# Moving filler work and VectorE's side work between the steps of a hand-ordered decoder layer

## The chip, the cores and the metric

The kernel runs on one core of one Trainium2 chip. The metric is the device time of one execution in microseconds (us); the time of a kernel is the median over its runs. The profile is of one further execution, recorded by the hardware profiler.

## The reference

One transformer layer in fp32 on 16 sequences of 512 tokens with 256 features. Cut to what matters:

```python
q = query @ wq + query @ Aq @ Bq * 4      # k, v alike; 16 heads of 16 features
q, k = rope(q), rope(k)
attn = softmax(where(causal, -1e9, q @ k.T / 4))
x = layernorm(query + (attn @ v) @ wo)
h = butterfly(x @ W_exp + b_exp, up_weights)        # 10 stages on 1024 features
h = butterfly(gelu(h + up_bias), down_weights)
out = layernorm(x + h @ W_con + b_con + down_bias)
```

Both butterflies are linear, so the kernel folds them into the two matrices once, in the first steps, and then computes `gelu(x @ W1 + b) @ W2`.

## The kernel before

The work is cut into steps, and the order of every engine's work is written out by hand. A batch (one sequence) takes 20 steps, `per = PER_QUAD * NQ`, in four quads of five steps; a quad is half of the heads of one chunk `c` of 128 features (`par` 0 or 1). A step has a slot 0 to 4 within its quad. Slots 0 and 1 treat 512 columns of scores for a pair of heads, slots 2 and 3 treat 384 + 128, slot 4 treats 256 + 256 for both pairs.

Two streams run through the steps, the second 15 steps (three quads) behind the first:

- `largest` computes scores into the PSUM tile `pa` (L421) and VectorE reduces each row of them to its largest (L430, the tiles `junk` and `mx`). One reduction is two instructions: a custom operation that reads the scores and a short read of the accumulator.
- `weights` computes transposed scores into `pb` (L479); ScalarE takes the exponential into `pT` (L493) and GpSimd zeroes the part above the diagonal (L497).

`pa` and `pb` have one buffer each, so TensorE can write the next step's scores only when VectorE and ScalarE have read those of this one. In slot 4 both tiles hold scores of both streams. After the scores of a step TensorE gets other work, which fills the time until the tiles are free again. Such fillers are:

- `weigh` (L521): probabilities times v, into `po`.
- `project_v` (L383): the product that makes v of one 128-token tile, into `pvv`; ScalarE copies it out (L391), in the last batch VectorE does.
- `contract` (L660): one half (four of eight chunks) of the second feed-forward product of a token tile, into `py`. After the second half VectorE adds the residual (L668) and takes the statistics (L577, L578).
- `project_out` (L559): the attention's output product, into `pwo`; VectorE adds the residual (L567) and takes the statistics.
- `hidden` (L633), `project` (L337) and the transposes `turn_x1` (L616) and `place_largest` (L448, tile `ptm`).

All filler tiles share three PSUM banks (`ps_w`).

VectorE's side work hangs on the same steps. `normalize(b, c, t)` inverts the softmax sums of one token tile (L553) and multiplies the attention output by them (L554); `project_out` of that tile needs the result. `spread` (L589, then a power on GpSimd, L590) and `offset` (L595) turn the statistics into scale and offset of the layer norm, which `centre` applies on ScalarE (L602).

GpSimd also does the rotary products and sums of the batch that comes next (L362, L365, L367 in `turn`), one per step, behind its L497 of that step.

`add(step, f, ...)` appends a function to the list `others[step]`. In a step come first the scores of both streams, then the reductions and exponentials, then `weigh`, then `others[step]` in the order of appending, then `holes[step]`. Each engine runs its instructions in that order. Batches are scheduled one after the other in a loop, so what an earlier batch put into a step stands ahead of what a later one puts there. In that loop `s` is the first step of batch `b`, and the tuples `at` are steps relative to it. A step relative to `s` modulo 20 is its place in the batch, and modulo 5 its slot.

Of the kernel before, what the change touches and what calls it, by code (L numbers as in the profile page):

```python
# [17 lines left out]
P = 128  # L18
# [15 lines left out]
def decoder_layer(  # L34
# [18 lines left out]
    nc = tc.nc  # L53
    B, T, D = x.shape
# [405 lines left out]
    state = {}  # L460
# [86 lines left out]
            nc.sync.dma_start(rows_of(sums, 1), rows_of(x, 0))  # L547
            nc.sync.dma_start(rows_of(even, 1), rows_of(x, 1))

    def normalize(b, c, t):  # L550
        x, sums = state["heads", b, c]
        ts = slice(t * P, (t + 1) * P)
        nc.vector.reciprocal(sums[:, ts], sums[:, ts])  # L553
        nc.vector.tensor_tensor(x[:, ts], x[:, ts], sums[:, ts], ALU.mult)  # L554

    def project_out(b, t):
        pw = bank(f"pwo_{b}_{t}", [P, D])
        for c in range(NC):
            nc.tensor.matmul(  # L559
                pw,  # L560
                state["heads", b, c][0][:, t * P : (t + 1) * P],
                wo_sb[:, c, :],
                start=(c == 0),
                stop=(c == NC - 1),
            )
        z = zs[b]
        nc.vector.tensor_add(z[:, t, :], pw, z[:, t, :])  # L567
        stats_of(1, b, t)
# [23 lines left out]
    def offset(which, b, t0=0, t1=NT):  # L592
        stats, norm = state["stats", which, b], state["norm", which, b]
        ts = slice(t0, t1)
        nc.vector.scalar_tensor_tensor(  # L595
            norm[:, 2, ts], stats[:, ts, 0], -1.0, norm[:, 1, ts], ALU.mult, ALU.mult
        )
# [30 lines left out]
    def hidden(b, hc, fused=False):  # L628
        if hc == 0:
            state["h", b] = hpool.tile([P, NHC, T], F32, tag="h", name=f"h_{b}")  # L630
        ph = bank(f"ph_{b}_{hc}", [P, T])
        for c in range(NC):
            nc.tensor.matmul(  # L633
                ph,
                wup[:, c, hc * P : (hc + 1) * P],
                state["x1T", b][:, c, :],
                start=(c == 0),
                stop=(c == NC - 1),
            )
        h = state["h", b][:, hc, :]  # L640
        if fused:
            nc.scalar.activation(h, ph, AF.Gelu, bias=hbias[:, hc : hc + 1])
        elif hc % 4 == 0:
            nc.vector.tensor_copy(h, ph)
        else:
            nc.scalar.copy(h, ph)  # L646

    def gelus(b, count=NHC):
        h = state["h", b]
        for hc in range(count):  # L650
            nc.scalar.activation(
                h[:, hc, :], h[:, hc, :], AF.Gelu, bias=hbias[:, hc : hc + 1]
            )
# [36 lines left out]
    others = {s: [] for s in range(-head, last)}  # L690
# [3 lines left out]
    def add(s, f, *args):  # L694
        others[s].append(lambda: f(*args))

    def start_projection(b, side, c):
        state["pr", b, side, c] = project(b, side, c)
# [13 lines left out]
    for b in range(B):  # L712
        s = b * per
        if b > 0:

            at = {1: (-16, -11, -13, -9), B - 1: (-1, 4, 10, 10)}.get(b, (-3, -1, 4, 14))
            for t in range(NT):
                add(s + at[t], project_v, b, t)
        if b + 1 < B:

            add(s - head * (b == 0), load_xT, b + 1)
            at = {0: (2, 5, 7, 10), 1: (3, 6, 8, 11)}.get(b, (10, 10, 10, 10))
            for i, (c, side) in enumerate(chains):
                holes.setdefault(s + at[i], []).append(
                    lambda b=b, side=side, c=c: start_projection(b + 1, side, c)
                )
                turning = s + max(at[0] + 1 + 3 * i, at[i] + 1)
                for step in range(3):
                    add(turning + step, turn, b + 1, side, c, step)
                for step in range(1 + side):  # L730
                    add(turning + (6 if i == 3 else 4) + step, part, b + 1, side, c, step)
        add(s + 9, load_x, b)
        add(s + 11, place_largest, b, 0)
        add(s + 21, place_largest, b, 1)
        for c in range(NC if b + 1 < B else 1):
            for t in range(NT):
                at = (27, 28, 29, 31) if c == 0 else (36, 37, 39, 40)
                add(s + (at[t] if b + 1 < B else 29 + t), normalize, b, c, t)
        if b + 1 < B:
            for t in range(NT):  # L740
                add(s + 41 + t // 2, project_out, b, t)
            add(s + 42, spread, 1, b)
            add(s + 43, offset, 1, b)
            add(s + 44, centre, 1, b)
            for c in range(NC):
                add(s + 45 + (b + 2 == B), turn_x1, b, c)
        if b + 2 < B:

            late = 2 * (b + 3 == B)
            for hc in range(NHC - late):  # L750
                add(s + 46 + hc // 2, hidden, b, hc)
            holes.setdefault(s + 50, []).insert(0, lambda b=b, late=late: gelus(b, NHC - late))
            for hc in range(NHC - late, NHC):
                holes[s + 50].append(lambda b=b, hc=hc: hidden(b, hc, True))
            for t in range(NT):
                for half in range(2):
                    at = (11, 12, 13, 15, 16, 18, 20, 23)[2 * t + half]
                    if b + 3 == B and t == NT - 1:
                        at = (23, 25)[half]
                    add(s + 40 + at, contract, b, t, half)  # L760
            add(s + 63 + 2 * (b + 3 == B), spread, 2, b)
            add(s + 67, offset, 2, b)
            add(s + 68, centre, 2, b)
            add(s + 68, store, b)
# [15 lines left out]
    for t in range(NT):  # L780
        add(end + 2, normalize, z, NC - 1, t)
# [206 lines left out]
```

## Time and profile before

| | |
|---|---|
| runs | 1358.62, 1364.54, 1364.14 us |
| median | 1364.14 us |
| profiled execution | 1357.15 us |
| its span | 1355.4 us |
| TensorE clock granted | 0.993 |
| TensorE busy | 1320.3 us, 97% of the span |
| TensorE weight loads | 702.5 us, 52% |
| VectorE busy | 925.8 us, 68% |
| ScalarE busy | 707.3 us, 52% |
| GpSimd busy | 510.9 us, 38% |
| DMA | 63.49 MB, 47 GB/s on average |

In lines of the timeline the first number is the start in us from the beginning of the span, the second the duration in us, then engine, source line, operation, and output and input tiles with their sizes; x2 means two merged instructions, whose common time is given. A bracket names idle time of the engine before the line and what ended it. PE is TensorE, PEld its weight loads, DVE VectorE, ACT ScalarE, POOL GpSimd. A matmul's displayed end is modelled and overlaps the next one's start, so lengths of steps are taken from start to start. On VectorE an instruction is often shown to start some 0.08 us ahead of the end of the one before it. The chain of waits is followed back from the last instruction, at each step to what released it.

### The profile page before, as it was taken

How to read it: one execution, taken by the hardware profiler on the slowest of the kernel's cores; microseconds unless marked ns; L12 is line 12 of the kernel's file. 1: busy time of each engine (PE TensorE's matmuls, PEld its weight loads, DVE VectorE, ACT ScalarE, POOL GpSimd, SP SyncE). 2: the span in 40 equal slices, each digit the busy share in tenths (PEclk: the TensorE clock that was granted, in tenths of full speed). 3: DMA queues.
4: the chain of work that ended last, by engine and by line, in shares of the span. 5: the costliest groups of instructions: out<-in, count | busy, mean ns of one | idle time of the engine just before them, and what ended most of it. 6: DMA issues, size and time to landing. Idle time of an engine off the chain costs nothing.

```text
span 1355.4 us, 23859 instructions
## 1 busy us (share of the span) xinstructions
PE 1320.3 (97%) x8728; PEld 702.5 (52%) x8728; DVE 925.8 (68%) x2949; ACT 707.3 (52%) x1079; POOL 510.9 (38%) x777
## 2 busy tenths in 40 slices
PE   8898999999999999999999999999999999998998
PEld 4453545455454545555454554545555454554555
DVE  4788757667685766758577685857768685776632
ACT  2575454454646445464645545464554546445643
POOL 3534215344251533425153352515335252531311
PEclk9998999999999999999999999999999999999999
DMA  5311010110102011010110101010110101000000
GB/s 172 120 45 45 22 59 30 40 45 30 68 30 74 30 41 45 30 67 30 67 35 31 57 30 68 30 60 30 40 60 30 68 30 55 30 27 32 30 12 31
DMA packets 45685, 63.49 MB, mean 47 GB/s; under 512 B 5752, under 2 KB 26232, under 8 KB 45568
## 3 DMA queue, kind: packets, MB, share of 16 engines
q1 hardware_dynamic: 41680, 56.42, 11.8%
q10 hardware_dynamic: 3888, 5.55, 1.3%
q8 instruction: 69, 1.13, 0.3%
q14 instruction: 48, 0.39, 0.1%
HBM read 23.40 MB, written 8.91 MB: 24 GB/s over the span
## 4 chain that ended last, share of the span: by engine, by line
PE 84%; DVE 11%; ACT 3%; issue 2%; DMA 0%; POOLq 0%; POOL 0%; DVEq 0%; SPq 0%; ACTq 0%
PE pb L479 19%; PE ph L633 17%; PE py L660 16%; PE po L521 10%; PE pqk L337 8%; DVE junk L430 5%; PE pvv L383 4%; PE pwo L559 3%; PE pa L421 3%; DVE bn L577 1%; PE pb L421 1%; PE pt L616 1%; ACT pT L493 1%; PE pa L479 1%; DVE z L567 1%
## 5 line engine op out<-in xcount | busy, mean ns | idle before, releaser
L430 DVE CUSTOM_DVE_ANT_0 junk<-pa,causal 128x384 bf16<-128x384 f32 (+2 forms) x878 | 438.3, 499 | 235.0 <-PE pa L421 176.1
L493 ACT ACTIVATE pT<-pb 128x1024 f32<-128x1024 f32 (+1 forms) x314 | 293.8, 936 | 377.3 <-PE pa L421 227.6
L497 POOL TENSOR_SCALAR_AFFINE_SELECT pT<-pT 128x256 f32<-128x256 f32 x512 | 202.5, 407 | 733.3 <-ACT pT L493 731.6
L479 PE MATMUL pb<-qz,kz 17*128 17x512 f32 (+2 forms) x1756 | 328.8, 473 | 16.1 <-ACT pT L493 12.1
L421 PE MATMUL pa<-kz,qz 32*128 32x384 f32 (+3 forms) x1756 | 329.2, 474 | 4.2 <-DVE mx L430 4.2
L660 PE MATMUL py<-wdn,h 128*128 128x256 f32 x1024 | 252.1, 391 | 0.0
L479 PEld LDWEIGHTS pb<-qz,kz 17*128 17x128 f32 (+1 forms) x1756 | 142.9, 183 | 179.5 <-issue 82.2
L633 PE MATMUL ph<-x1T,yb 128*128 128x512 f32 x512 | 235.8, 604 | 0.0
L660 PEld LDWEIGHTS py<-wdn,h 128*128 128x128 f32 x1024 | 185.1, 189 | 72.2 <-issue 36.2
L521 PE MATMUL po<-pT,vaug 128*32 128x512 f32 (+3 forms) x2048 | 179.5, 446 | 0.0
L633 PEld LDWEIGHTS ph<-x1T,yb 128*128 128x128 f32 x512 | 92.4, 189 | 122.3 <-issue 97.6
L421 PEld LDWEIGHTS pa<-kz,qz 32*128 32x128 f32 (+1 forms) x1756 | 143.7, 184 | 13.6 <-DVE mx L430 11.2
L553 DVE RECIPROCAL sums<-sums 128x128 f32<-128x128 f32 x128 | 121.1, 946 | 0.0
L337 PE MATMUL pqk<-xT,wqk 128*128 128x512 f32 x256 | 118.5, 613 | 0.0
L646 ACT COPY h<-ph 128x512 f32<-128x512 f32 x84 | 49.2, 585 | 123.2 <-PE ph L633 123.2
L521 PEld LDWEIGHTS po<-pT,vaug 128*32 128x32 f32 x2048 | 47.1, 109 | 102.3 <-issue 78.2
L430 DVE DVE_READ_ACCUMULATOR2_ANT mx<- 128x1 f32 x1024 | 84.5, 82 | 0.0
L337 PEld LDWEIGHTS pqk<-xT,wqk 128*128 128x128 f32 x256 | 48.0, 194 | 61.9 <-issue 57.4
L365 POOL TENSOR_TENSOR swap<-swap,rope_sb 128x512 f32<-128x512 f32 x62 | 79.6, 1283 | 0.0
L602 ACT ACTIVATE z<-z,norm 128x256 f32<-128x256 f32 x128 | 66.7, 589 | 24.6 <-DVE norm L595 24.5
L668 DVE TENSOR_TENSOR z<-py,z 128x256 f32<-128x256 f32 x64 | 27.1, 423 | 74.1 <-PE py L660 73.9
L430 DVE CUSTOM_DVE_ANT_0 junk<-pb,causal 128x256 bf16<-128x256 f32 (+3 forms) x146 | 63.6, 436 | 17.3 <-PE pa L421 4.0
(91 smaller groups left out, 1334.2 us busy)
## 6 DMA issues: line engine op xcount, KB each, us to landing
xT<-in_xT SPq DMA_DIRECT2D x16, 512.0 KB
swap<-qz SPq DMA_DIRECT2D x64, 128.0 KB
swap<-kz SPq DMA_DIRECT2D x64, 128.0 KB
z<-in_x SPq DMA_DIRECT2D x16, 512.0 KB
sums<-x SPq DMA_DIRECT2D x64, 128.0 KB
out_y<-z SPq DMA_DIRECT2D x15, 512.0 KB
x<-x SPq DMA_DIRECT2D x32, 128.0 KB
early<-in_wexpT ACTq DMA_DIRECT2D x1, 1028.0 KB
```

Source lines behind the costliest of these rows:

```text
L337: nc.tensor.matmul(pq, wqk[:, d, e : e + P], xTs[b][:, d, :], start=(d == 0), stop=(d == NC - 1))
L365: engine.tensor_tensor(swap, swap, rope_sb[:, 1, :], ALU.mult)
L421: lambda i=i, rows=rows, at=at, n=n, t=t, ps=ps: nc.tensor.matmul(ps[:, i, at : at + n], q[rows, par, t * P : n], k_[rows, par, 0:n], star ...
L430: lambda i=i, at=at, n=n, t=t, g=g, ps=ps: nc.vector.tensor_tensor_reduce(out=junk[:, 0:n], in0=ps[:, i, at : at + n], in1=causal[:, T - n ...
L479: lambda i=i, rows=rows, at=at, n=n, k=block, ps=ps: nc.tensor.matmul(ps[:, i, at : at + n], kt[rows, par, k * P : (k + 1) * P], qt[rows, ...
L493: nc.scalar.activation(pT[:, heads, 0:n], ps[:, :, at : at + n], AF.Exp)
L497: nc.gpsimd.affine_select(out=diag, in_=diag, pattern=[[0, 2], [1, P]], compare_op=ALU.is_ge, fill=0.0, base=0, channel_multiplier=-1,)
L521: nc.tensor.matmul(po[HG * g : HG * (g + 1), k * P : T], vaugs[b % 2][:, k, NG * c + g, first : first + HG], pT[:, g, at : at + n], start= ...
L553: nc.vector.reciprocal(sums[:, ts], sums[:, ts])
L602: nc.scalar.activation(zs[b][:, t, :], zs[b][:, t, :], AF.Identity, bias=norm[:, 2, t : t + 1], scale=norm[:, 1, t : t + 1],)
L633: nc.tensor.matmul(ph, wup[:, c, hc * P : (hc + 1) * P], state["x1T", b][:, c, :], start=(c == 0), stop=(c == NC - 1),)
L660: nc.tensor.matmul(py, state["h", b][:, hc, t * P : (t + 1) * P], wdn[:, hc, :], start=(hc == 0), stop=(hc == NHC - 1),)
```

## The change

Four tuples of places are changed, `normalize` is split in two, and one function moves to the front of its step.

- v products: for most batches token tile 1 moves from step -1 to 0 and tile 3 from 14 to 12; for the last batch tile 0 moves from -1 to -3.
- Contraction halves: from places 11, 12, 13, 15, 16, 18, 0, 3 to places 11, 13, 14, 15, 16, 18, 19, 3 (steps 51 to 63 after the batch's first).
- Reciprocal and product: `invert` and `scale` are scheduled apart. For `c` = 0, token tile 3 moves from step 31 to 30. For `c` = 1 the reciprocals stay at 36, 37, 39, 40 and the products move to 39, 39, 40, 41, behind the reductions of these steps; 41 is also the step of the first two `project_out`.
- `offset(1, b)` is put first in step 43's list, so that VectorE runs it ahead of the residual add and statistics of `contract` (of an earlier batch), instead of behind them.

No operation is added or removed.

```diff
-    def normalize(b, c, t):
+    def invert(b, c, t):
+        sums = state["heads", b, c][1]
+        ts = slice(t * P, (t + 1) * P)
+        nc.vector.reciprocal(sums[:, ts], sums[:, ts])
+
+    def scale(b, c, t):
         x, sums = state["heads", b, c]
         ts = slice(t * P, (t + 1) * P)
-        nc.vector.reciprocal(sums[:, ts], sums[:, ts])
         nc.vector.tensor_tensor(x[:, ts], x[:, ts], sums[:, ts], ALU.mult)
+
+    def normalize(b, c, t):
+        invert(b, c, t)
+        scale(b, c, t)
...
-            at = {1: (-16, -11, -13, -9), B - 1: (-1, 4, 10, 10)}.get(b, (-3, -1, 4, 14))
+            at = {1: (-16, -11, -13, -9), B - 1: (-3, 4, 10, 10)}.get(b, (-3, 0, 4, 12))
             for t in range(NT):
                 add(s + at[t], project_v, b, t)
...
             for t in range(NT):
-                at = (27, 28, 29, 31) if c == 0 else (36, 37, 39, 40)
-                add(s + (at[t] if b + 1 < B else 29 + t), normalize, b, c, t)
+                if b + 1 == B:
+                    add(s + 29 + t, normalize, b, c, t)
+                    continue
+                add(s + ((27, 28, 29, 30), (36, 37, 39, 40))[c][t], invert, b, c, t)
+                add(s + ((27, 28, 29, 30), (39, 39, 40, 41))[c][t], scale, b, c, t)
         if b + 1 < B:
             for t in range(NT):
                 add(s + 41 + t // 2, project_out, b, t)
             add(s + 42, spread, 1, b)
-            add(s + 43, offset, 1, b)
+            others[s + 43].insert(0, lambda b=b: offset(1, b))
             add(s + 44, centre, 1, b)
...
             for t in range(NT):
                 for half in range(2):
-                    at = (11, 12, 13, 15, 16, 18, 20, 23)[2 * t + half]
+                    at = (11, 13, 14, 15, 16, 18, 19, 23)[2 * t + half]
                     if b + 3 == B and t == NT - 1:
                         at = (23, 25)[half]
                     add(s + 40 + at, contract, b, t, half)
```

## The prediction

> **What bounds the kernel now.** I read the chain of waits first, then TensorE's timeline over one batch in the middle of the run, then VectorE's and GpSimd's beside it.
>
> ```profile
> PE 84%; DVE 11%; ACT 3%; issue 2%; DMA 0%; POOLq 0%; POOL 0%; DVEq 0%; SPq 0%; ACTq 0%
> ```
>
> The chain of waits is TensorE with a tenth of VectorE in it: TensorE is nearly always fed, and stops where a score bank is still being read. I number the 20 steps of a batch as places 0 to 19 (step modulo 20; slot = place modulo 5). A step starts with its first `pb` product. TensorE's timeline at places 14 to 16:
>
> ```profile
> 608.51 1.13 PE L383 MATMUL pvv<-wv_sb,xT 128*128 128x256 f32 x4
> 609.67 0.70 PE L479 MATMUL pb<-qz,kz 17*128 17x512 f32 x2
> 609.80 0.70 PE L421 MATMUL pa<-kz,qz 32*128 32x512 f32 x2
> ...
> 611.42 1.99 PE L660 MATMUL py<-wdn,h 128*128 128x256 f32 x8
> 613.35 0.70 PE L479 MATMUL pb<-qz,kz 17*128 17x512 f32 x2
> 613.36 0.70 PE L421 MATMUL pa<-kz,qz 32*128 32x512 f32 x2
> ```
>
> After a v product in a last slot the next step comes 609.67 - 608.51 = 1.16 us later, 1.06 where nothing waits (618.42 to 619.48, place 17), and `pa` trails `pb` by 0.13 instead of 0.01. So such a boundary costs 0.10 + 0.12 us. A contraction half fills 613.35 - 611.42 = 1.93 us and leaves no gap. Now VectorE and GpSimd around place 1:
>
> ```profile
> 628.50 0.95 DVE L553 RECIPROCAL sums<-sums 128x128 f32<-128x128 f32 x1
> 628.55 1.27 POOL L362 TENSOR_TENSOR kz<-kz,rope_sb 128x512 f32<-128x512 f32 x1
> ...
> 629.48 0.48 DVE L554 TENSOR_TENSOR x<-x,sums 128x128 f32<-128x128 f32 x1
> ...
> 632.12 0.42 DVE L567 TENSOR_TENSOR z<-pwo,z 128x256 f32<-128x256 f32 x1
> 632.18 1.27 POOL L365 TENSOR_TENSOR swap<-swap,rope_sb 128x512 f32<-128x512 f32 x1
> ...
> 632.60 0.28 PE L448 MATMUL ptm<-ident,mx 128*32 128x128 f32 x1
> ```
>
> Two things matter here. `ptm` shares the bank of `pwo` t=0 and starts 0.06 us after L567 ends: L567 is on TensorE's path. And the product L554 takes 0.48 us here, while alone (665.37) it takes 0.29. It ends 0.14 after GpSimd's rope product at 628.55 (629.96 against 629.82). At 679.32 the same product meets a rope product that runs from 678.87 to 680.14:
>
> ```profile
> 679.32 0.97 DVE L554 TENSOR_TENSOR x<-x,sums 128x128 f32<-128x128 f32 x1
> ```
>
> It ends at 680.29, again 0.15 after GpSimd. So a VectorE operation with two SBUF inputs does not slow down beside a rope product, it stops until that ends; the reciprocal, one input, keeps 0.95 in both cases. The tiny offset L595, also two SBUF inputs, shows it most clearly:
>
> ```profile
> 1276.23 2.32 DVE L595 SCALAR_TENSOR_TENSOR norm<-stats,norm 128x4 f32<-128x4 f32 x1
> ```
>
> Its usual 0.15 became 2.32 beside L621 on GpSimd (1276.17, 2.37). Before the change the reciprocal ahead of each product covers most of a rope product; the product loses only some 0.2.
>
> **The change part by part.** Times within a step are from its start.
>
> *Contraction and v products, places 12, 14, 15.* Place 12 goes from 4.00 (599.31 to 603.31) to place 17's 3.13, which has the same content. Place 14 from 3.36 to 0.12 stall + 1.08 scores + 1.00 weighing + 1.93 = 4.13. Place 15 from 3.68 to 3.56, its 0.12 stall gone. 10.82 for 11.04: -0.22 us a batch. VectorE's last read in place 14 (3.26) lies under the longer step. ScalarE's copies of v (0.40) move to places 13 and 1, ahead of an exponential that starts at 1.17: hidden.
>
> *Places 19 and 0.* Place 19: 3.38 becomes 4.13, as above. Place 0: 3.67 - 0.12 - 1.93 + 1.06 = 2.68, but VectorE's reads end at 2.67 (place 10 shows it unhindered) and the next `pa` starts 0.05 later: 2.72. So 6.85 for 7.05.
>
> *Products t=0 and t=1 behind the reads of place 19.* They follow without a reciprocal between. VectorE's last read is issued at 3.17, GpSimd's rope product about 3.28. Who wins such a meeting is seen once with nearly this spacing:
>
> ```profile
> 130.76 1.90 DVE L239 SCALAR_TENSOR_TENSOR early<-early,coefs,x 128x257 f32<-128x257 f32 x2
> ...
> 130.87 1.49 POOL L367 TENSOR_TENSOR kz<-kz,swap 128x512 f32<-128x512 f32 x1
> ```
>
> The first of the two operations took its 0.48, GpSimd was stretched from 1.27 to 1.49 and ended 1.13 after it, and the second waited for that. So: first product 3.17 to 3.46, rope product to 4.59, second product to 4.73, reciprocal t=2 from 4.65, VectorE free at 5.52. Place 0's reads could start at 4.13 + 1.24 = 5.37: 0.15 late. Bounds: 0 (both win) and 0.37 (both lose). I take 0.15, since three such pairs in the trace all let GpSimd in between. Place 0 becomes 2.88, not 2.72.
>
> *Products t=2 and t=3 in places 0 and 1.* On time, t=2 would be issued at 2.59, 0.10 ahead of the rope product (2.69); 0.15 late it loses and ends at 3.96 + 0.15 = 4.11. Reciprocal t=3 follows to 4.98, so the reads of place 1 start at 4.90 - 2.88 = 2.02 instead of 1.24 and end at 3.45. Product t=3 now stands before L567; the rope product of this place (2.65 to 3.92) holds it until 4.07. L567: 3.99 to 4.41; `ptm` 4.47; next step 0.21 after: 4.68. Before, 3.28: +1.40. If both products win: 2.59 + 0.21, L567 to 3.22, step 3.49, +0.21. I take 1.40.
>
> *The offset first in place 4.* It is meant to help ScalarE's L602, but that stands behind two exponentials (the second ends 642.93) while the offset was ready at 641.49: gain 0. Its cost:
>
> ```profile
> 639.42 1.26 POOL L367 TENSOR_TENSOR kz<-kz,swap 128x512 f32<-128x512 f32 x1
> ...
> 640.00 0.42 DVE L668 TENSOR_TENSOR z<-py,z 128x256 f32<-128x256 f32 x1
> ```
>
> Moved to 640.00, the offset waits until about 640.70. L668, statistics, spread and the reads queue behind it. L668 starts 0.64 later; without the offset after the spread, the reads start 1.20 after L668 instead of 1.41: +0.43, or +0.57 if the spread keeps its 0.30. Place 4's reads were already last (they end 3.53, the next `pb` starts 3.63), so this goes to the step. I take 0.45; the lower bound is 0.
>
> *Reciprocal t=3 of c=0 to place 10, and pairs taken apart.* Place 10 lasts 8.70 and GpSimd is idle there; the first `pqk` copy comes about 0.15 later than at 3.67, while its bank is wanted again near 6.8: 0. A product starts 0.03 after its reciprocal ends, an unrelated operation 0.08 before: by these rows four pairs save 0.45 us of VectorE in places with slack: 0. The Trainium skill ("VectorE: DVE Perf Modes", section "The DRAIN you can't avoid") says that a semaphore between two VectorE operations costs nothing extra; by it even the 0.45 would not exist. The sum is the same by both.
>
> *Sum.* -0.22 - 0.20 + 0.16 + 1.40 + 0.45 = +1.59 a batch; products of batches 1 to 12 fall in places as above and batch 13's meet the same rope products: 13 x 1.59 = 20.7. Ends: batch 0 (steps 37 to 41, no contraction yet, so the v product's place is not refilled) about +0.7; batch 14 (step 320, two products and a reciprocal more ahead of L567, no rope product) +0.5; place 14 of the last batch -0.2. Total +21.7 on a span of 1355.4, that is 1378.9 on the profiled execution's 1357.15. The median of the runs lies 1364.14 - 1357.15 = 7.0 above that execution: 1385 to 1386, say 1385.
>
> The Trainium skill ("SBUF — State Buffer", section "Who interferes with whom") goes by who starts first: the later one blocks for the whole instruction. By it, were place 0 on time, t=2 would win and the sum would be that of the first rival; no row shows a product winning with 0.10.
>
> **The rivals** (on the runs' scale).
> 1. VectorE wins the meetings in places 0 and 1. Place 0 2.82, place 1 3.49: -0.22 - 0.10 + 0.21 + 0.45 = +0.34; 13 x 0.34 + 1 = +5.4: 1370. For: the margins are some 0.1 us. Against: place 0 is late by more than it can spare.
> 2. Not slower, the change as its words have it: the rope products fall clear of products and offset, so places 14, 15, 19, 0 gain and only product t=3 delays `ptm`: -0.42 + 0.21 = -0.21; -2.7: 1361. It decides if GpSimd's products in places 0, 1 come 0.1 later, and that of place 3 ends before 3.19. Against: in place 3 it overlaps by 0.7.
> 3. The products block, the offset doesn't: 13 x 1.14 + 1 = +15.8: 1380.
>
> **How the numbers follow.** Forecast 0.64, rivals 0.14, 0.12, 0.10. The forecast's own range is 1380 to 1391: lateness 0.37 gives 13 x 0.22 = +2.9, the spread 1.6, ends 1. Leaving out rival 2 and part of 1, the range is 1368 to 1391. Half a per cent (6.8 us) is about what can be told from no change: rival 1 straddles it, rival 2 lies within. Slower 0.64 + 0.10 + 0.05 of rival 1 = 0.79; same 0.09 of rival 1 + 0.09 of rival 2 = 0.18; faster the rest of rival 2, 0.03.
>
> **What would show it.** L554 near 1.3 us in places 19, 0 and 1; L595 near 0.8 in place 4; place 1 about 4.7 long with `ptm` behind L567, place 4 about 4.1; places 14 and 19 4.13, place 15 with `pa` 0.01 behind `pb`. It is wrong if L554 stays near 0.3 there, or place 1 near 3.5.

## The result: slower by about half a per cent, well under half of what was forecast

| | before | after |
|---|---|---|
| median, us | 1362.12 (8 runs) | 1370.22 (8 runs) |
| lowest and highest | 1358.62 to 1364.54 | 1359.79 to 1373.5 |
| profiled execution, its span | 1357.15, 1355.4 | 1359.79, 1358.1 |

The ratio is 1.0059, 95% interval [1.0038, 1.0079]: about 8 us. The forecast was +21 (1385; range 1368 to 1391). The profile after, page, first the busy times, then the chain of waits by engine and by line:

```profile
PE 1314.2 (97%) x8728; PEld 699.3 (51%) x8728; DVE 923.8 (68%) x2949; ACT 707.0 (52%) x1079; POOL 514.6 (38%) x777
...
PE 82%; DVE 13%; ACT 3%; issue 2%; DMA 0%; POOLq 0%; POOL 0%; DVEq 0%; ACTq 0%
PE pb L479 19%; PE ph L641 17%; PE py L668 16%; PE po L521 10%; PE pqk L337 8%; DVE junk L430 6%; PE pvv L383 3%; PE pa L421 2%; PE pwo L567 1%; DVE bn L585 1%; PE pb L421 1%; PE pt L624 1%; DVE z L575 1%; ACT pT L493 1%; PE pa L479 1%
```

VectorE's share of the chain goes from 11 to 13%; of its lines `junk` L430 goes from 5 to 6%, and the add of the output projection (`z` L575, L567 before) stands at 1% in both pages. GpSimd is busy 3.7 us longer with the same instructions: meetings with VectorE stretch it. The rest must be read place by place. The table is made from both traces: a place lasts from its first `pb` product to that of the next; medians over the steady batches, in us, places that moved by 0.05 or more. The whole batch is read from step to step.

| place | 0 | 1 | 4 | 12 | 14 | 15 | 19 | whole batch |
|---|---|---|---|---|---|---|---|---|
| before | 3.68 | 3.27 | 3.64 | 4.00 | 3.36 | 3.68 | 3.38 | 79.54 |
| after, 10 of 13 batches | 2.70 | 3.53 | 4.06 | 3.13 | 4.12 | 3.56 | 4.12 | 79.78 |
| after, 3 of 13 | 2.70 | 4.66 | 4.06 | 3.13 | 4.12 | 3.56 | 4.12 | 80.90 |

So there are two kinds of batch. (The third lost batch is the last of the 13; its v products stand elsewhere, and its place 0 takes 2.31.) Here is VectorE's and GpSimd's timeline of the usual one, from the end of place 19 (620.04 to 624.15) through place 0 (to 626.86) and place 1 (to 630.39):

```profile
623.21 1.56 DVE L558 TENSOR_TENSOR x<-x,sums 128x128 f32<-128x128 f32 x2
623.32 1.30 POOL L367 TENSOR_TENSOR qz<-qz,swap 128x512 f32<-128x512 f32 x1
...
625.55 0.62 DVE L430 CUSTOM_DVE_ANT_0 junk<-pa,causal 128x512 bf16<-128x512 f32 x1
...
626.22 0.69 DVE L430 CUSTOM_DVE_ANT_0 junk<-pa,causal 128x512 bf16<-128x512 f32 x1
...
626.83 0.29 DVE L558 TENSOR_TENSOR x<-x,sums 128x128 f32<-128x128 f32 x1
626.86 1.39 POOL L362 TENSOR_TENSOR kz<-kz,rope_sb 128x512 f32<-128x512 f32 x1
...
629.50 0.29 DVE L558 TENSOR_TENSOR x<-x,sums 128x128 f32<-128x128 f32 x1
629.50 1.41 POOL L365 TENSOR_TENSOR swap<-swap,rope_sb 128x512 f32<-128x512 f32 x1
629.70 0.41 DVE L575 TENSOR_TENSOR z<-pwo,z 128x256 f32<-128x256 f32 x1
```

The first pair of products (t=0, t=1) behaves as forecast: t=0 goes through, the rope product slips in, t=1 waits for its end (1.56 for the two). The reads of place 0 then start 1.40 into the step, 0.16 late. But the product t=2 is issued just ahead of the rope product, 626.83 against 626.86 (22 to 25 ns over the ten batches, 14 and 19 in two of the others), takes its unhindered 0.29, and GpSimd is stretched from 1.27 to 1.39. The same happens to t=3 in place 1, where the two starts show the same number. In the other three batches that meeting goes the other way; VectorE and GpSimd, then TensorE, in place 1 of one of them (from 1026.09):

```profile
1028.74 1.41 DVE L558 TENSOR_TENSOR x<-x,sums 128x128 f32<-128x128 f32 x1
1028.74 1.27 POOL L365 TENSOR_TENSOR swap<-swap,rope_sb 128x512 f32<-128x512 f32 x1
1030.08 0.41 DVE L575 TENSOR_TENSOR z<-pwo,z 128x256 f32<-128x256 f32 x1
...
1030.54 0.28 PE L448 MATMUL ptm<-ident,mx 128*32 128x128 f32 x1 [1.27 <-DVE z L575]
1030.76 0.59 PE L479 MATMUL pb<-qz,kz 32*128 32x384 f32 x2
```

Now the product has the 1.41 and GpSimd its 1.27. L575 comes 1.13 later, `ptm` waits 1.27 us for it, by name, and the step with it. To the two decimals of a timeline the two batches start alike; in the recorded nanoseconds VectorE starts between 2 ahead and 1 behind in the won ones, 5 to 6 behind in two of the lost ones (in the third, the last batch, it is 0.39 us behind).

The offset in place 4 (from 637.39), the timeline of VectorE and GpSimd:

```profile
637.00 1.26 POOL L367 TENSOR_TENSOR kz<-kz,swap 128x512 f32<-128x512 f32 x1
...
637.58 0.70 DVE L603 SCALAR_TENSOR_TENSOR norm<-stats,norm 128x4 f32<-128x4 f32 x1
638.20 0.41 DVE L676 TENSOR_TENSOR z<-py,z 128x256 f32<-128x256 f32 x1
...
639.41 0.42 DVE L430 CUSTOM_DVE_ANT_0 junk<-pa,causal 128x256 bf16<-128x256 f32 x1
```

It ends 0.02 after GpSimd, and the reads begin 2.02 into the step (1.60 before): place 4 is 0.42 longer.

Between the starts of steps 60 and 320 the two traces differ by 5.5 us. The first 60 steps take 2.9 less after; there the granted clock differs between executions (in the trace after it is 1.00 from 160 to 240 us, before 0.98; last section).

### The profile page after: what moved, and what is told of

Same layout as the page of the kernel before. It is cut to its first block, busy times and chain, and to the rows that moved or that the text cites. A ratio compares the mean times of both kernels' runs of the same rounds, so it can differ in the third digit from the quotient of the medians.

```text
span 1358.1 us, 23904 instructions
## 1 busy us (share of the span) xinstructions
PE 1314.2 (97%) x8728; PEld 699.3 (51%) x8728; DVE 923.8 (68%) x2949; ACT 707.0 (52%) x1079; POOL 514.6 (38%) x777
## 3 DMA queue, kind: packets, MB, share of 16 engines
q8 instruction: 69, 1.13, 0.3%
## 4 chain that ended last, share of the span: by engine, by line
PE 82%; DVE 13%; ACT 3%; issue 2%; DMA 0%; POOLq 0%; POOL 0%; DVEq 0%; ACTq 0%
PE pb L479 19%; PE ph L641 17%; PE py L668 16%; PE po L521 10%; PE pqk L337 8%; DVE junk L430 6%; PE pvv L383 3%; PE pa L421 2%; PE pwo L567 1%; DVE bn L585 1%; PE pb L421 1%; PE pt L624 1%; DVE z L575 1%; ACT pT L493 1%; PE pa L479 1%
## 5 line engine op out<-in xcount | busy, mean ns | idle before, releaser
L430 DVE CUSTOM_DVE_ANT_0 junk<-pa,causal 128x384 bf16<-128x384 f32 (+2 forms) x878 | 437.6, 498 | 273.4 <-PE pa L421 231.4
L430 DVE DVE_READ_ACCUMULATOR2_ANT mx<- 128x1 f32 x1024 | 84.5, 82 | 0.0
L430 DVE CUSTOM_DVE_ANT_0 junk<-pb,causal 128x256 bf16<-128x256 f32 (+3 forms) x146 | 63.6, 435 | 15.8 <-PE pb L421 2.3
L383 PE MATMUL pvv<-wv_sb,xT 128*128 128x256 f32 x256 | 71.4, 403 | 0.0
```

Source lines behind the costliest of these rows:

```text
L383: nc.tensor.matmul(pv, xTs[b][:, d, t * P : (t + 1) * P], wv_sb[:, d, :], start=(d == 0), stop=(d == NC - 1),)
L430: lambda i=i, at=at, n=n, t=t, g=g, ps=ps: nc.vector.tensor_tensor_reduce(out=junk[:, 0:n], in0=ps[:, i, at : at + n], in1=causal[:, T - n ...
```

## The experiments

Each run was timed in five rounds beside the kernel before on the same chip. "Batch" is the steady batch from the run's trace, read as above, the won one where there are both; "lost" counts batches whose place 1 took 4.6 or more, of 13; the last batch is among them wherever it is not 0.

### First set: the two meetings, and repeats

`after_again` is the changed kernel once more.

> The changed kernel once more. Theory A (a meeting that goes either way): in the changed kernel's profile product t=3 of place 1 and GpSimd's rope product (L365) start within 6 ns of each other; in ten batches VectorE got in first (place 1 lasts 3.53 us), in three GpSimd did (4.66). The runs differ in how many of 13 batches are lost, so they spread over up to 13 x 1.13 = 15 us: median near 1370, single runs from 1359 to 1374. Theory B (granted clock alone): each run has about as many lost batches as the profile, and the spread follows the granted clock; the runs of before would then show the same low clocks and spread as far. Either way 1.004 to 1.008 of before.

`nudge_win` lets GpSimd do a tiny fill before the rope product of place 1, `nudge_lose` lets VectorE do one before the product t=3. `tick` is a new 128x1 tile that nothing reads; the edits are to the changed kernel.

```diff
+            if side == 1 and c == 1 and b > 1:          # nudge_win, in turn
+                nc.gpsimd.memset(tick, 0.0)
...
+        if c == 1 and t == NT - 1 and b + 1 < B:        # nudge_lose, in scale
+            nc.vector.memset(tick, 0.0)
```

> The changed kernel with one GpSimd memset of 128x1 (about 0.1 us by L153) ahead of the rope product of place 1, so that GpSimd comes later there. Theory A: VectorE wins in all 13 batches, place 1 lasts 3.53 us everywhere; against the changed kernel's profile 3 x 1.13 = 3.4 us less, span about 1354.7, and the runs lose the long ones: 0.998 to 1.002 of before, median about 1362. Theory B: the three batches are won too, but the median falls only by 3.4 us, to 1.002 to 1.006 of before.

> The changed kernel with one VectorE memset of 128x1 (about 0.06 us) ahead of product t=3 of place 1, so that VectorE comes later there. Theory A: GpSimd wins in all 13 batches, place 1 lasts 4.66 us everywhere: 10 x 1.13 = 11.3 us above the changed kernel's profile, span about 1369.5; the median of the runs rises little, to 1371 to 1375 (1.008 to 1.012 of before), with a narrower spread. Theory B: the median rises by the same 11 us above the changed kernel's, to 1.013 to 1.016 of before.

`products_back` joins the reciprocals and products again, at their old steps, and keeps the fillers and the offset of the change.

```diff
-                add(s + ((27, 28, 29, 30), (36, 37, 39, 40))[c][t], invert, b, c, t)
-                add(s + ((27, 28, 29, 30), (39, 39, 40, 41))[c][t], scale, b, c, t)
+                add(s + ((27, 28, 29, 31), (36, 37, 39, 40))[c][t], normalize, b, c, t)
```

> The changed kernel with reciprocal and product of c=1 together again in steps 36, 37, 39, 40 (and c=0 tile 3 in 31); contraction halves, v products and the offset stay moved. Theory A: place 1 falls from 3.53 or 4.66 to about 3.3, place 0 stays near 2.75; per batch -0.22 (places 12 to 15) -0.2 (19, 0) +0.43 (4) +0.1: +0.1 us, within 0.3% of before, and no wide spread. If the products are not what makes the changed kernel's runs long, it stays at 1.004 to 1.008.

| run | median, us | ratio to before, interval | batch | lost |
|---|---|---|---|---|
| before, same chip | 1360.53 | | 79.54 | 0 |
| after_again | 1365.59 | 1.0044 [1.0027, 1.0061] | 79.78 | 3 |
| nudge_win | 1363.44 | 1.0013 [0.9995, 1.0031] | 79.78 | 1 |
| nudge_lose | 1375.94 | 1.0112 [1.0089, 1.0136] | 80.90 | 13 |
| products_back | 1362.16 | 1.0016 [0.9996, 1.0037] | 79.68 | 0 |

The two nudges, one instruction each, lie 0.99% apart, 13.5 us: 12 batches by 1.13. So the winner of the meeting in place 1 is worth that. VectorE's and GpSimd's timeline there, first a batch of `nudge_win`, then one of `nudge_lose`:

```profile
716.58 0.10 POOL L367 MEMSET tick<- 128x1 f32 x1
716.61 0.29 DVE L561 TENSOR_TENSOR x<-x,sums 128x128 f32<-128x128 f32 x1
716.64 1.38 POOL L368 TENSOR_TENSOR swap<-swap,rope_sb 128x512 f32<-128x512 f32 x1
```

```profile
637.46 1.26 POOL L366 TENSOR_TENSOR swap<-swap,rope_sb 128x512 f32<-128x512 f32 x1
637.47 1.40 DVE L561 TENSOR_TENSOR x<-x,sums 128x128 f32<-128x128 f32 x1
637.49 0.06 DVE L560 MEMSET tick<- 128x1 f32 x1
```

GpSimd's fill put the start of the rope product 34 to 39 ns behind that of VectorE's product, which won all twelve steady batches. VectorE's fill, though 59 ns long and ahead in VectorE's order, moved the product by about 9 ns (it then started 8 to 12 ns behind the rope product, 14 in one batch), and that lost the meeting every time. `after_again` has three lost batches, like the first profile; apart from the last batch, where VectorE is 0.39 us late and loses in every kernel that has the meeting at its place, they are other ones. So it is a draw of nanoseconds, batch by batch. The ratios of both nudges lie in the ranges that theory A gave. But `nudge_lose` is 10.4 us above `after_again` and `nudge_win` 2.2 below, near theory B's 11 and 3.4, where theory A had the median rise little and fall by 8. So a typical run has few of its batches lost, not nearly all; how many, one trace a kernel doesn't show. The spread of the runs goes with the granted clock, as theory B had it (last section). `products_back` bears its expectation out: place 1 took 3.37, and no meeting was lost. So what the changed kernel loses in place 1 comes with the split products.

### Second set: each edit alone, or undone

`places_only`, `offset_only` and `products_only` are the kernel before with one part of the change each:

```diff
-            at = {1: (-16, -11, -13, -9), B - 1: (-1, 4, 10, 10)}.get(b, (-3, -1, 4, 14))      # places_only
+            at = {1: (-16, -11, -13, -9), B - 1: (-3, 4, 10, 10)}.get(b, (-3, 0, 4, 12))
...
-                    at = (11, 12, 13, 15, 16, 18, 20, 23)[2 * t + half]
+                    at = (11, 13, 14, 15, 16, 18, 19, 23)[2 * t + half]
```

```diff
-            add(s + 43, offset, 1, b)                                                          # offset_only
+            others[s + 43].insert(0, lambda b=b: offset(1, b))
```

```diff
-                at = (27, 28, 29, 31) if c == 0 else (36, 37, 39, 40)                          # products_only
-                add(s + (at[t] if b + 1 < B else 29 + t), normalize, b, c, t)
...
+                add(s + ((27, 28, 29, 30), (36, 37, 39, 40))[c][t], invert, b, c, t)
+                add(s + ((27, 28, 29, 30), (39, 39, 40, 41))[c][t], scale, b, c, t)
```

`offset_back` is the changed kernel with the second of these undone:

```diff
-            others[s + 43].insert(0, lambda b=b: offset(1, b))
+            add(s + 43, offset, 1, b)
```

`ptm_first` is the changed kernel with

```diff
-        add(s + 21, place_largest, b, 1)
+        others[s + 21].insert(0, lambda b=b: place_largest(b, 1))
```

> Only the filler places change (contraction halves and v products); products, reciprocals and offset stand as in the kernel before. Theory 'the three edits add up': places 12, 14 and 15 give -0.21 us per batch as in the profile of the changed kernel (3.13, 4.12, 3.56 us against 4.00, 3.36, 3.68), places 19 and 0 together give another -0.1 to -0.24, no meeting on the way of place 1 is lost (place 1 stays at 3.27), place 4 stays at 3.63: batch of 79.54 goes to 79.1 to 79.25, times 13 is -4 to -6 us, ratio to before 0.9955 to 0.997. Rival 'the filler moves bring the loss': places 19, 0, 1 are late in the same way without the split products, the batch is 79.6 or more, ratio 1.000 to 1.004.

> Only the offset is put first in its step. Theory 'blocked offset': it takes 0.70 us in place of 0.15, place 4 goes from 3.63 to 4.06 us in all 13 batches, no other place moves: +0.43 x 13 = +5.5 us, ratio to before 1.004. Rival 'hidden': place 5 gives back what place 4 loses, ratio 1.000.

> Only the reciprocals are parted from their products; fillers and the offset stand as before. Theory 'the fillers' places set who comes first': place 19 is 3.38 instead of 4.12 us there, so VectorE, blocked by the rope product of place 19 until about 1.55 us, has 0.7 us less to catch up and issues the product t=2 after the rope product of place 0: lost, place 1 goes from 3.27 to 4.4 to 4.7 us in all batches, batch 80.7 to 81.0, ratio 1.009 to 1.013. Rival 'the split costs nothing or little by itself': VectorE wins as in the changed kernel, batch 79.5 to 79.9, ratio 0.999 to 1.004.

> The changed kernel with the offset back at its old place in the step. Theory 'the three edits add up': place 4 is 3.63 again, -0.43 x 13 = -5.5 us against the changed kernel; a won batch is 79.32 (before 79.54), and with 3 of 13 batches lost at +1.13 the sum against before is -2.8 + 3.4 = +0.6 us: ratio 0.999 to 1.002. Rival 'the offset's delay decides the later meeting in place 1 too': the number of lost batches changes clearly (0 or over 8 of 13) and the ratio leaves that range (0.997 or 1.006 and more).

> The changed kernel with the spread-and-largest product of place 1 (its ptm) issued first in its step instead of after the output projection, so that it no longer waits for the bank that VectorE's addition frees. Theory 'bank': where the meeting is lost, place 1 goes from 4.66 to about 3.6 us and place 2 stays near 4.0; ratio to before 1.000 to 1.003. Theory 'VectorE's own queue': VectorE is as late as before and its reads of place 2 are what ends place 2, so that what place 1 gains place 2 loses: places 1 and 2 together stay at 7.5 us in won batches and 8.7 in lost ones, ratio 1.003 to 1.006.

| run | median, us | before | ratio, interval | batch | lost |
|---|---|---|---|---|---|
| places_only | 1356.71 | 1359.40 | 0.9976 [0.9957, 0.9995] | 79.25 | 0 |
| offset_only | 1367.19 | 1359.40 | 1.0052 [1.0033, 1.0071] | 79.96 | 0 |
| products_only | 1362.55 | 1358.69 | 1.0035 [1.0022, 1.0049] | 79.72 | 1 |
| offset_back | 1361.42 | 1359.40 | 1.0012 [0.9995, 1.0029] | 79.35 | 3 |
| ptm_first | 1365.59 | 1359.40 | 1.0050 [1.0032, 1.0068] | 79.69 | see text |

The edits add up. The filler places gain 0.29 a batch, the offset costs 0.42, the products cost 0.10 on top of the new places (79.35 against 79.25) where every meeting is won, together 0.23; and each lost batch costs 1.13. In the trace after, with two of the twelve steady batches lost, that is 12 x 0.23 + 2 x 1.13 = 5.0; one place 4 that took 0.34 more, as in five of the other traces (why is open), and 0.14 for the last batch make it the 5.5 us between steps 60 and 320, 0.41%. Measured were 0.44 and 0.59%. In `places_only` place 1 took 3.37, not the 3.27 expected. `offset_only` is the blocked-offset theory in full: place 4 at 4.06 in the steady batches and nothing given back in place 5.

`products_only` missed its theory. The product t=2 did meet a running rope product there, as expected; VectorE's and GpSimd's timeline in places 0 (629.44 to 633.11) and 1:

```profile
632.13 1.27 POOL L362 TENSOR_TENSOR kz<-kz,rope_sb 128x512 f32<-128x512 f32 x1
...
632.89 0.66 DVE L558 TENSOR_TENSOR x<-x,sums 128x128 f32<-128x128 f32 x1
...
634.35 0.69 DVE L430 CUSTOM_DVE_ANT_0 junk<-pa,causal 128x512 bf16<-128x512 f32 x1
...
635.70 0.29 DVE L558 TENSOR_TENSOR x<-x,sums 128x128 f32<-128x128 f32 x1
635.76 1.35 POOL L365 TENSOR_TENSOR swap<-swap,rope_sb 128x512 f32<-128x512 f32 x1
```

But place 0 is 3.68 long there, with a contraction half in it, so VectorE is through before the reads of place 1 begin at 1.24, and t=3 wins by 60 ns. The batch is the rival's (79.5 to 79.9), its reason is not: VectorE lost at t=2. In these two kernels being lost is dear where the step is short.

`ptm_first` bears out neither theory as it stood. In its one lost meeting of the twelve steady batches place 1 stayed at 3.45 and place 2 at 4.00: the bank was what held place 1. But VectorE's reads of place 2 began 1.13 late, and the lateness came out in the next two places, +0.38 in place 3 and +0.63 in place 4, 1.01 of the 1.13 (the lost last batch shows the same, +0.31 and +0.62). VectorE's queue was the limit after all, further on than expected.

### Third set: the forecast's own branch

Was the forecast's price right, had the product t=2 in place 0 lost? Three attempts, all edits of `scale` in the changed kernel: `lose_t2` puts the 128x1 fill ahead of t=2, `lose_t2_more` a 128x128 fill, `lose_t2_four` four 128x1 fills.

```diff
+        if c == 1 and t == NT - 2 and b + 1 < B:
+            for n in range(4):                          # lose_t2_four
+                nc.vector.memset(tick[:, n : n + 1], 0.0)
```

> The changed kernel with one small VectorE fill (128x1) in front of the product t=2 of place 0, which so comes some 60 ns later, more than its lead of 22 to 25 ns before the rope product. Theory of the forecast's branch: that product is lost (about 1.4 us in place of 0.29), the reads of place 1 start near 2.0 us, the product t=3 waits for the same end of a rope product as before, place 1 ends near 4.68 us in all 13 batches and place 0 stays near 2.7: batch 80.9, as where only t=3 is lost, ratio to before 1.010 to 1.013. Rival 'the two losses add': place 1 takes 3.53 + 2 x 1.13 = 5.8 us, batch 82.0, ratio 1.020 to 1.024. Rival 'no loss': the product wins all the same and the batch stays at 79.8, ratio 1.004.

> As lose_t2, where the 128x1 fill moved the product t=2 of place 0 by 8 ns only and its lead of 22 to 25 ns was not used up; here the fill is 128x128, estimated at 50 to 150 ns more by the rows of the VectorE copies and products of that size, so that the product comes after the rope product of place 0. Forecast's branch: product t=2 lost (about 1.4 us), reads of place 1 from about 2.0 us, product t=3 blocked by the rope product of place 1 until 4.07, place 1 at 4.66 to 4.70 us in all 13 batches: batch 80.9, ratio to before 1.010 to 1.013, a median near 1373. Rival 'the losses add': place 1 near 5.8, batch 82.0, ratio 1.020 to 1.024. Rival 'it hardly matters': t=2 is lost but t=3 is not blocked, place 1 stays under 3.8, ratio 1.004 to 1.006.

> As lose_t2_more, with four fills of 128x1 in place of one of 128x128: the large fill itself was not blocked (0.165 us, begun 35 ns after the rope product) and the product behind it ran in 0.228 us, so that the product t=2 was never lost. Four small fills put it some 100 to 250 ns behind the rope product of place 0 (8 ns for the first, 59 ns for each further one by the duration of one). Forecast's branch: product t=2 is blocked until the rope product's end (about 1.2 to 1.3 us), place 1 is 4.66 to 4.70 us in all 13 batches: batch 80.9, ratio to before 1.010 to 1.013. Rival 'the losses add': place 1 near 5.8, batch 82.0, ratio 1.020 to 1.024. Rival 'fills keep the way open': the product is not blocked, place 1 stays under 3.8 in most batches, ratio 1.003 to 1.006.

| run | median, us | before | ratio, interval | batch | lost |
|---|---|---|---|---|---|
| lose_t2 | 1364.02 | 1358.69 | 1.0054 [1.0032, 1.0076] | 79.78 | 4 |
| lose_t2_more | 1362.01 | 1358.97 | 1.0032 [1.0013, 1.0050] | 79.77 | 1 |
| lose_t2_four | 1378.17 | 1360.43 | 1.0131 [1.0102, 1.0159] | 80.90 | 13 |

`lose_t2` failed as a test: the fill took 8 ns of the lead where 60 were expected, and t=2 still won everywhere. `lose_t2_more` failed in another way; VectorE and GpSimd in place 0:

```profile
628.18 1.47 POOL L363 TENSOR_TENSOR kz<-kz,rope_sb 128x512 f32<-128x512 f32 x1
628.21 0.17 DVE L560 MEMSET tick<- 128x128 f32 x1
628.29 0.23 DVE L561 TENSOR_TENSOR x<-x,sums 128x128 f32<-128x128 f32 x1
```

The product begins 0.11 behind the rope product and isn't blocked; GpSimd is stretched to 1.47. `lose_t2_four` did what was wanted, from place 0 (its end is 557.88) to the next L579 of place 1:

```profile
557.89 1.27 POOL L363 TENSOR_TENSOR kz<-kz,rope_sb 128x512 f32<-128x512 f32 x1
...
557.91 1.40 DVE L562 TENSOR_TENSOR x<-x,sums 128x128 f32<-128x128 f32 x1
...
560.09 0.62 DVE L431 CUSTOM_DVE_ANT_0 junk<-pa,causal 128x512 bf16<-128x512 f32 x1
...
560.53 1.27 POOL L366 TENSOR_TENSOR swap<-swap,rope_sb 128x512 f32<-128x512 f32 x1
...
561.38 0.58 DVE L562 TENSOR_TENSOR x<-x,sums 128x128 f32<-128x128 f32 x1
561.88 0.41 DVE L579 TENSOR_TENSOR z<-pwo,z 128x256 f32<-128x256 f32 x1
```

The product t=2 is lost by 10 ns or so (not by the 100 to 250 expected: the four fills moved it by some 35), and everything behind it is the forecast's chain: reads of place 1 late, t=3 held to the end of the rope product, place 1 4.66 in all steady batches. The losses do not add, since t=3 waits for the same end of a rope product either way.

### The best version

`best` is `places_only` with the `ptm` of `ptm_first` and the fourth reciprocal and product of the lower chunk at step 30; against `places_only`:

```diff
-        add(s + 21, place_largest, b, 1)
+        others[s + 21].insert(0, lambda b=b: place_largest(b, 1))
...
-                add(s + ((27, 28, 29, 31), (36, 37, 39, 40))[c][t], normalize, b, c, t)
+                add(s + ((27, 28, 29, 30), (36, 37, 39, 40))[c][t], normalize, b, c, t)
```

> The kernel before with the filler places of the change alone, the ptm of place 1 first in its step, and the fourth reciprocal and product of the lower chain a step earlier (place 10 instead of 11 of the next half), as the changed kernel has it. Theory: 79.24 us per batch with the filler places alone, -0.08 from place 1 (3.53 to 3.45 where ptm was first), -0.05 from places 13 and 14 (3.00 and 4.12 in place of 3.09 and 4.07): 79.1, against 79.54 before -0.43 x 13 = -5.6 us, ratio 0.995 to 0.998. Rival: the moves bring a new wait of the size they save, ratio 0.998 to 1.001.

Measured: 1354.65 us median (1352.56 to 1362.24, 12 runs) against 1358.69, ratio 0.9972 [0.9954, 0.9990]; batch 79.29 (79.1 was expected), no batch lost. It is faster than the kernel before, and so than the changed one. Its two extras brought nothing: `ptm` in front makes place 1 3.45, longer than the 3.37 of `places_only`, and the earlier reciprocal and product gain 0.04 in places 13 and 14. `places_only`, 0.9976, is the same within the intervals, with less done to the code.

## Why the prediction was right in direction and wrong in size

**Right: places 12, 14, 15.** Forecast -0.22, measured -0.23, with 3.13, 4.12 and 3.56 against 3.13, 4.13 and 3.56.

**Right: the offset.** Forecast 0.70 for it and +0.45 for place 4; 0.70 and +0.42 measured, alone and in the whole.

**Right: products t=0 and t=1 at place 19.** First through, rope product between, second blocked, reads of place 0 late by 0.15 (0.16).

**Partly wrong: places 19 and 0.** Their 0.16 of lateness did not lengthen place 0, which took 2.70, not 2.88. A place lasts from `pb` to `pb`, and VectorE's late reads held only `pa`: it stands 0.12 behind `pb` in place 1; so a won place 1 is 3.53, not rival 1's 3.49. Together places 19 and 0 gained 0.23 where the sum had 0.04. The sum's 13th batch, too, is not like the others: it grew by 0.14 in place of 1.59, as its place 0 went from 3.71 to 2.31.

**Wrong: "0.15 late it loses".** This is the step that failed. On time, t=2 would be issued at 2.59, the rope product at 2.69; 0.15 was added to the one and nothing to the other. In the trace the first read, 0.16 late, took 0.62 instead of 0.69, so the second read and the product were only 0.09 late: 2.68. The rope product came at 2.705. So of the 75 ns or so between forecast and measurement about 60 are VectorE's and 15 GpSimd's.

With t=2 won, the reciprocal and the reads of place 1 stay near their time, and the next meeting, t=3, is a tie within 6 ns in twelve batches of the first profile, of which VectorE won ten. So +1.40 a batch became +0.26, or +1.39 in three of 13. The forecast's own sign of being wrong, the product near 0.3 and place 1 near 3.5, is what the ten show.

The price itself was right. `lose_t2_four` puts place 1 at 4.66 (forecast 4.68), the second blocked product's end at 561.38 + 0.58 - 557.88 = 4.08 (4.07), and the run at 1.0131: 17.8 us, near the +21.7 (of the difference 2.5 are places 19 and 0, about 1 is the last batch). What was mis-called is who wins: forecast 50 ns behind, measured 22 to 25 ns ahead in the ten won batches. Given the other winner, the first rival's sum stood on record, +5.4 or 1370, with a chance of 0.14. That the median came to 1370.22 is partly luck: a won batch cost 0.23, not the rival's 0.34, the rival had no meeting lost, and the runs of before came to 1362.12 in place of 1364.14. The spacing of 0.05 between 2.74 and 2.69 deserved nearly even chances, and the read's duration was taken as fixed while it was not.

**Rivals 2 and 3.** Rival 2 (nothing blocks) fell with the offset and t=1, both blocked. Rival 3 (products block, offset doesn't) fell with the offset.

The Trainium skill ("SBUF — State Buffer", section "Who interferes with whom") says that for a VectorE operation with two SBUF inputs and a GpSimd operation that reads SBUF issue order decides, and the later one is fully blocked. The runs agree where starts are apart (won at 22 to 25 ns ahead, lost at 0.39 and 0.75 us behind). Within a few ns the shown start doesn't tell: products 3 to 5 ns behind won in some runs (`ptm_first`), and two 3 ns behind lost in another (`lose_t2`). And the product of `lose_t2_more`, 0.11 us behind by the shown starts, was not blocked; there the measurement decides, and the rule by shown starts does not hold. The wait, too, is shorter than the shown times say: GpSimd, 22 to 25 ns behind a product of 0.29, was stretched by 0.12.

## What to carry to other kernels

Where two engines exclude each other, compare their issue times to some 10 ns and follow lateness through every instruction between; if the forecast of the gap is smaller than the errors of its terms, give both outcomes even chances and price both. Put operations that can be blocked into steps with room behind them: a product lost in place 0 cost 1.1 us where that step lasts 2.70, and at most the 0.2 by which place 1 grew where it lasts 3.68. And test the parts of a bundle one by one: here the filler places alone were a gain of 0.2 to 0.3% that an offset moved into another engine's way (0.42 a batch) had more than eaten.

## What the runs showed of the hardware that was not expected

**Behind a large fill the product was not blocked.** A 128x128 fill, begun some 35 ns after the rope product's shown start, took 0.165 us, and the two-input product behind it took 0.23 and was not blocked, in all 13 batches; 128x1 fills (59 ns each, but 8 to 9 ns of delay each) did not do that: behind one of them t=3 was blocked in all 13 batches of `nudge_lose`, behind four t=2 in all 13 of `lose_t2_four`. Why the large fill does is open; it wasn't tried by itself.

**A read that starts late is shorter.** The first reduction of place 0 took 0.62 instead of 0.69 when it began 0.16 late, and so did the late read of place 1 in `lose_t2_four`. Why it is 0.07 shorter was not tried.

**The runs differ in the first 240 us.** A stretch of the trace per row: length, busy times, then granted clock, DMA share and GB/s. First `offset_back` (mean clock 0.987), then the kernel before (0.993):

```profile
40.00:80.00 40.00, 36.13 (x209) 19.64 (x206) 26.28 (x93) 27.22 (x64) 16.04 (x19) 0.87 0.23 74
80.00:160.00 80.00, 72.52 (x502) 36.74 (x501) 63.80 (x194) 44.70 (x89) 29.77 (x47) 0.91 0.13 44
160.00:240.00 80.00, 77.52 (x523) 40.63 (x525) 54.47 (x168) 39.14 (x56) 28.95 (x43) 0.98 0.11 38
240.00:700.00 460.00, 458.55 (x3115) 241.20 (x3107) 316.69 (x1035) 246.83 (x360) 182.34 (x269) 1.00 0.13 45
```

```profile
40.00:80.00 40.00, 34.41 (x239) 18.88 (x238) 29.93 (x107) 29.02 (x70) 17.21 (x19) 1.00 0.29 93
80.00:160.00 80.00, 71.98 (x514) 37.05 (x506) 66.72 (x200) 43.47 (x83) 30.22 (x48) 0.94 0.11 38
```

Between 240 and 1280 us the clock is full in both. Before that it isn't, by amounts that vary: step 60 began between 225.2 us (mean clock of the run 0.994) and 234.1 (0.985) in the fifteen traces. These 9 us are of the size of the scatter between the runs of one kernel (before, in the second set: 1354.86 to 1364.31) and of the change's whole effect. The length of a batch with the same winners, read from the trace, nearly always repeats to 0.02 us; so the parts were weighed by batches here and the medians served as a check. They can be made a better one: over all timed runs here, a run is about 1.1 us longer than the mean of its kernel for each 0.001 of mean clock less. Set to one clock by this slope (an estimate), `after_again` lies 4 us above `nudge_win` and 9 below `nudge_lose`, as if some four of its batches were lost, and the gain of `best` against before is 2.6 us, that of `places_only` 3.5.
